# Degrees of a sorted graph from one comparison a group, and the edge loads of the last two groups on another queue

## The chip, the cores and the metric

The kernel runs on one core of one Trainium2 chip. A core has TensorE (PE in the profile, PEld its weight loads), VectorE (DVE), ScalarE (ACT), GpSimd (POOL) and SyncE (SP, which here only starts transfers). SP, ACT and POOL each own a queue on which transfers are issued; all transfers run on the core's 16 DMA engines. The metric is the device time of one execution in microseconds (us), lower is better; several executions are timed and their median counts.

## What is computed

Three graph convolutions with ReLU on 6250 nodes of 256 features and 100000 edges, then a residual sum and a layer norm. `src` and `dst` come sorted by `dst`.

```python
def _gcn_layer(h_in, W, b, src, dst, norm_edge, n_nodes):
    h = h_in @ W
    msg = h[src] * norm_edge[:, None]
    agg = jax.ops.segment_sum(msg, dst, num_segments=n_nodes)
    return agg + b
...
deg = jax.ops.segment_sum(jnp.ones_like(dst, dtype=x.dtype), dst, num_segments=n)   # with self loops
dinv = jnp.where(deg > 0, jax.lax.rsqrt(deg), 0.0)
norm_edge = dinv[src] * dinv[dst]
for W, b in ((W1, b1), (W2, b2), (W3, b3)):
    h = jax.nn.relu(_gcn_layer(h, W, b, src, dst, norm_edge, n))
...
x = _layernorm(x + h, axis=-1)
```

The part that matters here is `deg`: the number of edges that end in each node, plus one, and its use `dinv`, by which every row of x is scaled before the first layer can gather rows.

## The kernel before

**Blocks and groups.** The nodes are cut into NB = 50 blocks of Q = 125, and the blocks into NG = 5 groups of GRP = 10. A first part (up to line 1632) finds for each block where its edges start in the sorted list (`starts`). Then `sorted_path` runs. Its opening, the subject here, fills lines 554 to 717: it loads for each block a run of CAP = 2048 edges, 16 a partition (`ed`), counts the degrees of the nodes, scales x by `dinv` and stores the scaled x to a table in DRAM (`tables[0]`, shown as `tab`). After that come three layers, in which POOL gathers rows of the tables by edge (line 1186), PE sums them with one-hot matrices (1213), and counts of edges between blocks are made (`counts`, lines 785, 814, 852) for a dense product (1273).

**How a degree is counted** (`counted(g)`, lines 627 to 671, a generator with three stages). Partition p of a block holds 16 sorted destinations, made relative to the block in `dlo` (629). For each of 126 thresholds v the number of edges with a destination below v is wanted, and degrees are the differences of neighbours (`step`, 655). DVE makes `near` (values cut off at 125, less 128, line 632), its negative (633), `full` (partitions whose last value is below v, line 636) and `begun` (first value below v, line 638), each of the latter two over 128 x 1260 elements. PE then runs three matmuls a block (642 to 644): begun on near, full on minus near, full on ones. What is left in `part_ps` is, for each threshold, the values of the one partition in which the threshold lies; comparing them (649) and summing (651), plus 16 for each full partition (653), gives the count. Stage two ends with the square root on ACT (659). Stage three takes the reciprocal (661), scales the ten blocks of x (665 on DVE for odd blocks from the third group on, 667 on ACT) and issues the stores of five blocks at a time from SP (669, through `by_rows`, two transfers each, line 74).

**The order.** The whole opening is under a manual schedule: each engine runs its instructions in the order of the Python text. The loop at 704 calls, for k = 0 to 6, stage one of group k, stage three of group k - 2, stage two of group k - 1, and between them single steps of `search()`, which finds the windows of edges that the counts of the first layer need (lines 486 to 549; the matmuls 508 and 509, the sums 511, then an indirect load on POOL, line 521, and further DVE steps from 528). Then `in_parts` (673) splits the scaled x of groups three to five into `parts` (ACT line 675, DVE line 676); the first layer needs it, and the loads of biases and weights (1546, 1547, 756) and the stores of `both` (1439) come behind it on SP.

**The queues in the opening.** `load_edges` (559) reads a start into a register (561) and issues one transfer of 16 KB (564). Of each block group, blocks 0 to 3 are on SP, 4 to 7 on ACT, 8 and 9 on POOL; SP and ACT issue 20 of these each, POOL 10. Behind its 20, SP issues the loads of x of groups three to five (682; those of the first two groups are issued by ACT at the start, line 1568), then four small zero rows (688), then the stores. POOL issues two edge loads, then five indirect loads of edges beyond the 2048 of a block (`beyond`, line 609, used by `rest_counted` 613 in stage two of the first group), then the other eight edge loads.

Of the kernel before, what the change touches and what calls it, by code (L numbers as in the profile page):

```python
# [10 lines left out]
F32 = mybir.dt.float32  # L11
F32R = mybir.dt.float32r
BF16 = mybir.dt.bfloat16
# [9 lines left out]
P = 128  # L23
# [373 lines left out]
def sorted_path(ctx: ExitStack, tc: tile.TileContext, x, edges, starts, found, wts, biases, room, late, out):  # L397
# [156 lines left out]
    with tc.tile_pool(name="sdeg1", bufs=1) as dp1, tc.tile_pool(name="sdeg", bufs=2) as dp, \  # L554
# [17 lines left out]
        base_i = dp1.tile([P, NB], I32, name="base_i")  # L572
        low_i = dp1.tile([P, 2], I32, name="slow_i")
        low = dp1.tile([P, 2], F32, name="slow")
        ones_b = dp1.tile([P, 1], BF16, name="ones_b")
        step = dp1.tile([P, Q], F32, name="step")
        eps = const.tile([P, 1], F32, name="seps")
        zero = dp1.tile([1, HID], F32, name="szero")
# [3 lines left out]
        hot_rest = dp1.tile([P, NG, Q], BF16, name="hot_rest")  # L582

        def numbers():
            nc.gpsimd.iota(low_i, pattern=[[-P, 2]], base=0, channel_multiplier=1)
            nc.gpsimd.iota(base_i, pattern=[[Q, NB]], base=0, channel_multiplier=0)
            nc.gpsimd.iota(keys_i, pattern=[[1, G * NB]], base=0, channel_multiplier=0)
            make_identity(nc, same)
            nc.gpsimd.iota(own_i, pattern=[[0, 1]], base=0, channel_multiplier=G)
            nc.gpsimd.memset(ones_b, 1.0)  # L590
            nc.gpsimd.memset(eps, EPS)
            nc.gpsimd.memset(zero, 0.0)
            nc.vector.tensor_copy(low, low_i)
# [33 lines left out]
        def counted(g):  # L627
            gs = slice(g, g + GRP)
            nc.vector.tensor_tensor(dlo[:, gs, :KF], ed[:, gs, :, 1],
                                    base_i[:, gs].unsqueeze(2).to_broadcast([P, GRP, KF]), op=ALU.subtract)  # L630
            near = dp.tile([P, 2, GRP, KF], BF16, name="near")
            nc.vector.tensor_scalar(near[:, 0], dlo[:, gs, :KF], float(Q), float(P), op0=ALU.min, op1=ALU.subtract)
            nc.vector.tensor_scalar(near[:, 1], near[:, 0], -1.0, None, op0=ALU.mult)
            every = cols[:, :VS].unsqueeze(1).to_broadcast([P, GRP, VS])
            full = dp.tile([P, GRP, VS], BF16, name="sfull")
            nc.vector.tensor_tensor(full, every, dlo[:, gs, KF - 1:KF].to_broadcast([P, GRP, VS]), op=ALU.is_gt)
            begun = dp.tile([P, GRP, VS], BF16, name="begun")
            nc.vector.tensor_tensor(begun, every, dlo[:, gs, 0:1].to_broadcast([P, GRP, VS]), op=ALU.is_gt)
            part_ps = psd.tile([VS, GRP, KF], F32, name="part_ps")
            full_ps = psd.tile([VS, GRP], F32, name="full_ps")  # L640
            for b in range(GRP):
                nc.tensor.matmul(part_ps[:, b, :], lhsT=begun[:, b, :], rhs=near[:, 0, b, :], start=True, stop=False)
                nc.tensor.matmul(part_ps[:, b, :], lhsT=full[:, b, :], rhs=near[:, 1, b, :], start=False, stop=True)
                nc.tensor.matmul(full_ps[:, b:b + 1], lhsT=full[:, b, :], rhs=ones_b, start=True, stop=True)
            yield
            if g == 0:
                rest_counted()
            below = dp.tile([VS, GRP, KF], F32, name="sbelow")
            nc.vector.tensor_scalar(below, part_ps, low[:VS, 1:2], None, op0=ALU.is_lt)
            n_part = dp.tile([VS, GRP], F32, name="n_part")  # L650
            nc.vector.reduce_sum(n_part, below, axis=mybir.AxisListType.X)
            n_below = dp.tile([VS, GRP], F32, name="n_below")
            nc.vector.scalar_tensor_tensor(n_below, full_ps, float(KF), n_part, op0=ALU.mult, op1=ALU.add)
            deg_ps = psd.tile([Q, GRP], F32, name="sdeg_ps")
            nc.tensor.matmul(deg_ps, lhsT=step[:VS, :], rhs=n_below, start=True, stop=False)
            nc.tensor.matmul(deg_ps, lhsT=hot_rest[:, g // GRP, :], rhs=member[:, gs], start=False, stop=True)

            root = dp.tile([Q, GRP], F32, name="sroot")
            nc.scalar.activation(root, deg_ps, AF.Sqrt, bias=1.0)
            yield  # L660
            nc.vector.reciprocal(dinv[:, gs], root)
            v = x_of(g)
            for b in range(GRP):
                if g >= 2 * GRP and b % 2:
                    nc.vector.tensor_scalar(v[:, b, :], v[:, b, :], dinv[:, g + b:g + b + 1], None, op0=ALU.mult)
                else:
                    nc.scalar.activation(v[:, b, :], v[:, b, :], AF.Copy, scale=dinv[:, g + b:g + b + 1])
                if b % 5 == 4:
                    by_rows(nc.sync, v[:, b - 4:b + 1, :],
                            tables[0][(g + b - 4) * Q:(g + b + 1) * Q, :].rearrange("(b p) c -> p b c", p=Q), store=True)  # L670
            yield
# [4 lines left out]
            nc.vector.tensor_sub(parts[:, gs, C:], x_of(g), parts[:, gs, :C].bitcast(F32))  # L676

        with tc.manual_schedule():
            load_edges(SP, nc.sync, [g + b for g in range(0, NB, GRP) for b in range(4)])
            load_edges(ACT, nc.scalar, [g + b for g in range(0, NB, GRP) for b in range(4, 8)])  # L680
            for g in range(2 * GRP, NB, GRP):
                load_x(nc.sync, x_of(g), g)
            numbers()
            load_edges(POOL, nc.gpsimd, range(8, GRP))
            beyond()
            load_edges(POOL, nc.gpsimd, [g + b for g in range(GRP, NB, GRP) for b in range(8, GRP)])
            for table in (*tables, both_halves):
                nc.sync.dma_start(out=table[N:N + 1, :], in_=zero[:, :table.shape[1]])
            nc.vector.tensor_copy(cols, keys_i[:, :P])
            nc.vector.tensor_copy(ident_r, same)  # L690
            nc.vector.tensor_copy(loops, same)
            nc.vector.tensor_sub(step, ident[:, 1:Q + 1], ident[:, 0:Q])
            nc.vector.tensor_copy(own0, own_i)
            idle_slots = 0

            def search():
                nonlocal idle_slots
                if idle_slots > 0:
                    idle_slots -= 1
                else:  # L700
                    idle_slots = next(searches) // 2

            stages = [counted(g) for g in range(0, NB, GRP)]
            for k in range(NG + 2):
                for g in (k, k - 2, k - 1):
                    if 0 <= g < NG:
                        next(stages[g])
                        if k > 0:
                            search()
                if k == NG - 1:  # L710
                    nc.vector.tensor_copy(src, ed[:, :, :, 0])
            while not seen:
                next(searches)
            for g in range(2 * GRP, NB, GRP):
                in_parts(g)
            late_w()
            nc.vector.tensor_copy(keys, keys_i)
# [960 lines left out]
```

## Time and profile before

| | |
|---|---|
| median of 3 runs | 2073.05 us (2067.38 to 2081.36) |
| the profiled execution's own time | 2076.16 us |
| its span, first to last instruction | 2074.4 us |
| busy share: PE, DVE, POOL, ACT | 93%, 72%, 68%, 63% |
| mean granted TensorE clock | 0.961 |
| first gather of the first layer (POOL, line 1186) | starts at 72.95 us |
| first product of a gathered row (PE, line 1213) | starts at 88.14 us |

All sums are made against one profiled execution, whose time is 2076.16 us; that is 3.1 us above the median of the three runs. Times inside the trace are counted from the start of its span. In the rows, the first number is the start and the second the duration in us; what stands in square brackets is how long the engine was idle before, and what ended that.

### The profile page before, as it was taken

What the parts mean: (1) busy time and instruction counts of PE and PEld (TensorE: products, weight loads), DVE (VectorE), ACT (ScalarE), POOL (GpSimd) and SP (SyncE); (2) the same over time, 40 slices, a digit from 0 to 9 for tenths busy, and PEclk for the clock granted to TensorE, in tenths of its full rate; (3) what the DMA queues carried; (4) which work ended last, traced back from release to release, by engine and by line L of the source; (5) the groups of instructions that cost most, each with busy time, mean ns of one, the idle gap of its engine ahead of it and who ended that gap; (6) DMA issues with size and microseconds to landing.
All of it is one profiled execution on the core that took longest, in us unless ns stands there. A gap on an engine that the chain in (4) does not pass through costs nothing. (4 is left out here: it accounts for less than half of the span.)

```text
span 2074.4 us, 30032 instructions
## 1 busy us (share of the span) xinstructions
PE 1923.9 (93%) x8642; PEld 1513.7 (73%) x8642; DVE 1494.1 (72%) x2809; ACT 1302.3 (63%) x2484; POOL 1418.2 (68%) x1442
## 2 busy tenths in 40 slices
PE   4399999999999688999999999999989899999996
PEld 3277777777776467778888878887767777777774
DVE  6877888888882376777766777677675467777776
ACT  2576777787884465766766656667565455556553
POOL 2467777766777377777776776677674577777775
PEclk6699999999999899999999999999999999999998
DMA  7898999999999999999999998978886466666674
GB/s 172 244 308 212 271 260 256 276 260 257 275 274 252 264 268 248 269 260 265 261 262 258 258 260 239 266 230 266 244 239 189 115 180 183 182 178 190 174 191 117
DMA packets 233624, 486.17 MB, mean 234 GB/s; under 512 B 44142, under 2 KB 87358, under 8 KB 233446
## 3 DMA queue, kind: packets, MB, share of 16 engines
q0 software_dynamic: 125184, 315.61, 54.6%
q1 hardware_dynamic: 94980, 159.23, 27.9%
q10 hardware_dynamic: 13282, 9.30, 1.7%
q8 instruction: 70, 1.15, 0.2%
q14 instruction: 108, 0.88, 0.1%
HBM read 416.51 MB, written 67.47 MB: 233 GB/s over the span
## 5 line engine op out<-in xcount | busy, mean ns | idle before, releaser
L1186 POOL DMA_INDIRECT room<-tab,ssrc x1008 | 1025.8, 1018 | 384.6 <-issue 162.6
L1243 DVE TENSOR_TENSOR halves<-room,halves 128x512 fp32r<-128x512 f32 (+1 forms) x806 | 453.4, 579 | 279.0 <-ACT halves L1240 273.0
L1240 ACT CAST halves<-room 128x512 fp32r<-128x512 f32 (+1 forms) x806 | 408.5, 528 | 286.0 <-DMA room<-tab,ssrc 244.7
L1213 PE MATMUL sacc<-halves,shot 128*125 128x512 f32 x1541 | 527.1, 406 | 38.8 <-DVE shot L1136 27.8
L1186 POOL DMA_INDIRECT halves<-both,ssrc x384 | 360.5, 939 | 143.3 <-issue 41.8
L1213 PEld LDWEIGHTS sacc<-halves,shot 128*125 128x125 f32 x1541 | 286.9, 188 | 120.4 <-ACT halves L1240 25.1
L785 DVE TENSOR_TENSOR room<-near_cols,slots 128x625 bf16<-128x625 f32 (+2 forms) x435 | 325.3, 804 | 30.8 <-PE sacc L852 12.7
L1145 ACT CAST piece<-room 125x625 fp32r<-125x625 uint8 x416 | 297.2, 722 | 70.4 <-PE win_ps L1273 19.2
L1136 DVE TENSOR_TENSOR shot<-near_cols,sdlo 128x500 fp32r<-128x500 f32 x371 | 248.0, 670 | 9.3 <-PE sacc L1213 4.8
L1366 PE MATMUL win_ps<-room,w_sb 128*128 128x250 f32 (+1 forms) x832 | 192.5, 375 | 1.6 <-ACT room L1372 1.6
L1273 PE MATMUL win_ps<-parts,piece 125*125 125x512 f32 x650 | 186.2, 405 | 6.2 <-ACT piece L1145 6.2
L1273 PE MATMUL smm<-parts,piece 125*125 125x512 f32 x655 | 188.9, 405 | 1.3 <-ACT piece L1145 0.7
L1366 PEld LDWEIGHTS win_ps<-room,w_sb 128*128 128x128 f32 x832 | 158.0, 195 | 25.3 <-ACT room L1372 2.0
L1273 PE MATMUL mat_ps<-parts,piece 125*125 125x512 f32 x600 | 172.4, 404 | 1.3 <-ACT piece L1145 1.3
L852 PEld LDWEIGHTS <-room 128*125 128x125 bf16 x725 | 95.8, 138 | 74.0 <-issue 23.0
L1273 PE MATMUL sacc<-parts,piece 125*125 125x512 f32 x450 | 147.6, 432 | 0.9 <-ACT piece L1145 0.9
L1273 PEld LDWEIGHTS win_ps<-parts,piece 125*125 125x125 f32 x650 | 119.3, 188 | 37.7 <-ACT piece L1145 8.0
L814 ACT CAST room<-sacc 125x500 uint8<-125x500 f32 (+1 forms) x155 | 107.6, 712 | 56.5 <-PE sacc L852 41.7
L1273 PEld LDWEIGHTS smm<-parts,piece 125*125 125x125 f32 x655 | 116.8, 187 | 29.3 <-issue 2.3
L936 DVE TENSOR_TENSOR parts<-parts 125x512 fp32r<-125x512 f32 x150 | 103.4, 689 | 41.6 <-ACT parts L934 41.6
L1273 PEld LDWEIGHTS mat_ps<-parts,piece 125*125 125x125 f32 x600 | 107.6, 186 | 29.4 <-ACT piece L1145 3.0
L1243 DVE TENSOR_TENSOR parts<-room,parts 128x512 fp32r<-128x512 f32 x138 | 93.4, 692 | 33.3 <-ACT parts L1240 32.9
(310 smaller groups left out, 2938.5 us busy)
## 6 DMA issues: line engine op xcount, KB each, us to landing
parts<-tab SPq DMA_DIRECT2D x81, 448.0 KB
kept<-room SPq DMA_DIRECT2D x29, 683.6 KB
room<-kept SPq DMA_DIRECT2D x29, 683.6 KB
tab<-st SPq DMA_DIRECT2D x74, 224.0 KB
room<-tab,ssrc POOLq DMA_INDIRECT x1008
both<-parts SPq DMA_DIRECT2D x10, 1120.0 KB
own_row<-tab SPq DMA_DIRECT2D x38, 224.0 KB
parts<-kept SPq DMA_DIRECT2D x60, 136.7 KB
```

Source lines behind the costliest of these rows:

```text
L785: nc.vector.tensor_tensor(out, near_cols[:, :shape[2]].unsqueeze(1).to_broadcast(shape), numbers.unsqueeze(2).to_broadcast(shape), op=ALU. ...
L814: nc.scalar.copy(place[:, :, u * G:(u + len(ms)) * G].rearrange("p k (t r) -> p t k r", r=G), counted_in[:Q, :len(ms) * 256].rearrange("p ...
L852: nc.tensor.matmul(bank[:Q, len(pair) * 256:][:, :G * NB], lhsT=hot_lo, rhs=hot_key, start=True, stop=True)
L936: nc.vector.tensor_sub(to[:, HID:], row, to[:, :HID].bitcast(F32))
L1136: nc.vector.tensor_tensor(hot[:, :n], near_cols[:, :Q].unsqueeze(1).to_broadcast([P, n, Q]), dlo.rearrange("p b j -> p (b j)")[:, at:at + ...
L1145: convert(piece, made_or_read[:, c * PIECE:(c + 1) * PIECE, :])
L1186: nc.gpsimd.indirect_dma_start(out=row, out_offset=None, in_=table, in_offset=bass.IndirectOffsetOnAxis(ap=at, axis=0))
L1213: nc.tensor.matmul(acc[:Q, :size], lhsT=hot, rhs=row[:, c0:c0 + size], start=(i == 1 and k == c0 == 0), stop=(k == KF and c0 + size == row ...
L1240: nc.scalar.copy(halves[:, :width], landed[chunk - hi_lag])
L1243: nc.vector.tensor_sub(halves[:, width:], landed.pop(chunk - lo_lag), halves[:, :width].bitcast(F32))
L1273: nc.tensor.matmul(acc_d[:Q], lhsT=got[done // PIECE][:, k % PIECE, :], rhs=parts[:, k], start=(k == 0), stop=(k == NB - 1))
L1366: nc.tensor.matmul(h_ps[:, f, :], lhsT=w2_sb[:, k, (f2 + f) * P:(f2 + f + 1) * P], rhs=zt[:, k, :], start=(k == 0), stop=(k == KH - 1))
```

## The change

It has two parts.

*The count.* `full`, the negative of `near` and the third matmul of each block go. `near` is now the values cut off at 125, plus 1. A new 128 x 128 matrix `shift` (ones on the diagonal, minus ones beside it, first column special) turns, in one matmul for the whole group (`rise_ps`), the values of all partitions into their rises over the partition before. DVE copies these rises from PSUM to a bf16 tile `steps_of[...]`, which has a 17th column of ones for each block. One matmul a block, `begun` on the 17 columns, then sums the rises of all partitions that have begun; the sum is the values of the last of them, and the 17th column counts the partitions. `shift` and the ones are made once.

*The queues.* SP and ACT issue the edge loads of the first three groups only (12 each instead of 20), so that SP's loads of x come behind the third group's edges. POOL issues blocks 8 and 9 of the first two groups (4 loads), then the five indirect loads, then blocks 28 and 29 and all twenty blocks of the last two groups (22 loads).

```diff
@@ constants
-        ones_b = dp1.tile([P, 1], BF16, name="ones_b")
+        shift = dp1.tile([P, P], BF16, name="shift")
+        steps_of = [dp1.tile([P, GRP, KF + 1], BF16, name=f"steps_of{n}") for n in range(2)]
...
-            nc.gpsimd.iota(low_i, pattern=[[-P, 2]], base=0, channel_multiplier=1)
+            nc.gpsimd.iota(low_i, pattern=[[1, 2]], base=0, channel_multiplier=1)
...
-            nc.gpsimd.memset(ones_b, 1.0)
+            for rises in steps_of:
+                nc.gpsimd.memset(rises[:, :, KF:], 1.0)
@@ counted(g)
-            near = dp.tile([P, 2, GRP, KF], BF16, name="near")
-            nc.vector.tensor_scalar(near[:, 0], dlo[:, gs, :KF], float(Q), float(P), op0=ALU.min, op1=ALU.subtract)
-            nc.vector.tensor_scalar(near[:, 1], near[:, 0], -1.0, None, op0=ALU.mult)
+            near = dp.tile([P, GRP, KF], BF16, name="near")
+            nc.vector.tensor_scalar(near, dlo[:, gs, :KF], float(Q), 1.0, op0=ALU.min, op1=ALU.add)
             every = cols[:, :VS].unsqueeze(1).to_broadcast([P, GRP, VS])
-            full = dp.tile([P, GRP, VS], BF16, name="sfull")
-            nc.vector.tensor_tensor(full, every, dlo[:, gs, KF - 1:KF].to_broadcast([P, GRP, VS]), op=ALU.is_gt)
             begun = dp.tile([P, GRP, VS], BF16, name="begun")
             nc.vector.tensor_tensor(begun, every, dlo[:, gs, 0:1].to_broadcast([P, GRP, VS]), op=ALU.is_gt)
-            part_ps = psd.tile([VS, GRP, KF], F32, name="part_ps")
-            full_ps = psd.tile([VS, GRP], F32, name="full_ps")
+            rise_ps = psd.tile([P, GRP, KF], F32, name="rise_ps")
+            nc.tensor.matmul(rise_ps, lhsT=shift, rhs=near, start=True, stop=True)
+            rises = steps_of[g // GRP % 2]
+            nc.vector.tensor_copy(rises[:, :, :KF], rise_ps)
+            part_ps = psd.tile([VS, GRP, KF + 1], F32, name="part_ps")
             for b in range(GRP):
-                nc.tensor.matmul(part_ps[:, b, :], lhsT=begun[:, b, :], rhs=near[:, 0, b, :], start=True, stop=False)
-                nc.tensor.matmul(part_ps[:, b, :], lhsT=full[:, b, :], rhs=near[:, 1, b, :], start=False, stop=True)
-                nc.tensor.matmul(full_ps[:, b:b + 1], lhsT=full[:, b, :], rhs=ones_b, start=True, stop=True)
+                nc.tensor.matmul(part_ps[:, b, :], lhsT=begun[:, b, :], rhs=rises[:, b, :], start=True, stop=True)
...
-            nc.vector.scalar_tensor_tensor(n_below, full_ps, float(KF), n_part, op0=ALU.mult, op1=ALU.add)
+            nc.vector.scalar_tensor_tensor(n_below, part_ps[:, :, KF], float(KF), n_part, op0=ALU.mult, op1=ALU.add)
@@ the loads
-            load_edges(SP, nc.sync, [g + b for g in range(0, NB, GRP) for b in range(4)])
-            load_edges(ACT, nc.scalar, [g + b for g in range(0, NB, GRP) for b in range(4, 8)])
+            first_groups = range(0, 3 * GRP, GRP)
+            load_edges(SP, nc.sync, [g + b for g in first_groups for b in range(4)])
+            load_edges(ACT, nc.scalar, [g + b for g in first_groups for b in range(4, 8)])
             for g in range(2 * GRP, NB, GRP):
                 load_x(nc.sync, x_of(g), g)
             numbers()
-            load_edges(POOL, nc.gpsimd, range(8, GRP))
+            load_edges(POOL, nc.gpsimd, [g + b for g in (0, GRP) for b in range(8, GRP)])
             beyond()
-            load_edges(POOL, nc.gpsimd, [g + b for g in range(GRP, NB, GRP) for b in range(8, GRP)])
+            load_edges(POOL, nc.gpsimd, [*range(2 * GRP + 8, NB)])
...
+            nc.vector.tensor_copy(shift[:, 0:1], same[:, 0:1])
+            nc.vector.tensor_sub(shift[:, 1:], same[:, 1:], same[:, :P - 1])
```

More of the change, by code (lines that the diff above doesn't have):

```diff
@@ L648, in counted @@
             below = dp.tile([VS, GRP, KF], F32, name="sbelow")
-            nc.vector.tensor_scalar(below, part_ps, low[:VS, 1:2], None, op0=ALU.is_lt)
+            nc.vector.tensor_scalar(below, part_ps[:, :, :KF], low[:VS, 1:2], None, op0=ALU.is_lt)
             n_part = dp.tile([VS, GRP], F32, name="n_part")
```

## The prediction

> **What bounds the kernel now.** I read the page first, then the stretches, then the engines in order of time up to 92 us.
>
> ```profile
> span 2074.4 us, 30032 instructions
> PE 1923.9 (93%) x8642; PEld 1513.7 (73%) x8642; DVE 1494.1 (72%) x2809; ACT 1302.3 (63%) x2484; POOL 1418.2 (68%) x1442
> ...
> PE   4399999999999688999999999999989899999996
> ```
>
> Each digit of the last line is a slice of 52 us. From the third slice on PE is nearly full: the layers are bound there and the change does not touch them. Only the first 90 us can move, and what moves there shifts everything behind it once. So the question is what ends the opening last.
>
> ```profile
> 20.00:25.00 5.00, 2.84 (x27) 2.84 (x28) 2.11 (x2) 0.00 (x0) 4.39 (x5) 0.50 0.42 42
> 31.00:50.20 19.20, 15.13 (x109) 13.60 (x110) 16.47 (x38) 9.01 (x24) 0.00 (x0) 0.50 1.04 233
> 50.20:68.30 18.10, 7.20 (x42) 5.76 (x42) 13.09 (x42) 14.52 (x24) 1.30 (x1) 0.50 0.95 289
> 72.00:90.00 18.00, 4.58 (x14) 3.40 (x15) 16.87 (x21) 3.55 (x5) 12.69 (x10) 0.50 0.97 296
> ```
>
> These are stretches: length, busy us of PE, PEld, DVE, ACT, POOL, then granted clock, DMA share, GB/s. Up to 31 us the DMA engines are half empty, behind that they are full, and DVE is busy 86% of 31 to 50. Two chains run side by side. The first is SP's:
>
> ```profile
> 13.71 16.60 SPq L564 DMA_DIRECT2D ed<-in_edges  x20
> 30.36 3.90 SPq L76 DMA_DIRECT2D room<-in_x  x4
> 34.31 6.03 SPq L76 DMA_DIRECT2D last_x<-in_x  x2
> 64.23 4.03 SPq L74 DMA_DIRECT2D tab<-last_x  x4
> 71.92 11.89 SPq L74 DMA_DIRECT2D both<-parts  x6
> ...
> SPq L74 <- DMA last_x<-in_x: 5.4, 1, 5.4
> ...
> L74 SPq DMA_DIRECT2D tab<-room x14: 310/760/1615, 50.2 to 63.6; - x14
> ```
>
> Twenty edge loads take SP 0.83 us each (16.60 / 20); the loads of x start only behind them. One store then waits 5.4 us for the last load of x to land, and from 50.2 us all further stores run with full DMA engines. The last is issued at 68.3. POOL's first gather follows it:
>
> ```profile
> 72.95 2.14 POOL L1186 DMA_INDIRECT room<-tab,rest  x1 [17.75 <-DMA b_sb<-in_L_gnn_b]
> 75.40 0.95 POOL L1186 DMA_INDIRECT room<-tab,ssrc  x1 [0.30 <-issue]
> ...
> 88.14 1.19 PE L1213 MATMUL mat_ps<-room,shot 128*125 128x256 f32 x2 [4.29 <-DMA room<-tab,ssrc]
> ...
> 91.19 2.24 DVE L785 TENSOR_TENSOR room<-near_cols,slots 128x625 bf16<-128x625 f32 x3 [2.09 <-PE str L852]
> ```
>
> PE waits for the gathered row, and DVE then waits 2.09 us for PE: where the chains meet, SP's is the later one by about 2.1 us. The second chain is DVE's:
>
> ```profile
> 27.19 0.33 DVE L629 TENSOR_TENSOR sdlo<-ed,base_i 128x160 f32<-128x160 int32 x1 [5.09 <-DMA ed<-in_edges]
> 46.37 0.33 DVE L629 TENSOR_TENSOR sdlo<-ed,base_i 128x160 f32<-128x160 int32 x1 [0.30 <-issue]
> 60.69 0.23 DVE L528 TENSOR_SCALAR w_sb<-w_sb 125x128 f32<-125x128 int32 x1 [0.66 <-DMA w_sb<-in_edges,w_sb]
> 65.94 5.56 DVE L676 TENSOR_TENSOR parts<-room,parts 125x2560 fp32r<-125x2560 f32 x2 [2.34 <-ACT parts L675]
> ```
>
> At 27.19 it waits for edges of the second group; the fifth group's count starts at 46.37.
>
> **The change part by part.**
>
> ```profile
> L636 DVE TENSOR_TENSOR sfull<-scols,sdlo 128x1260 bf16<-128x1260 f32 x5 | 7.3, 1465 | 0.0
> L633 DVE TENSOR_SCALAR near<-near 128x160 bf16<-128x160 bf16 x5 | 1.0, 202 | 0.2
> L649 DVE TENSOR_SCALAR sbelow<-part_ps,slow 126x160 f32<-126x160 f32 x5 | 1.8, 365 | 0.0
> L692 DVE TENSOR_TENSOR step<-ident_r 128x125 f32<-128x125 f32 x1 | 0.3, 286 | 0.0
> L643 PE MATMUL part_ps<-near,sfull 128*126 128x16 bf16 x50 | 12.7, 254 | 0.0
> L852 PE MATMUL sacc<-room 128*125 128x250 bf16 x34 | 8.2, 308 | 16.8 <-DVE room L785 16.4 <-DVE w_sb L513 0.3
> ```
>
> *DVE.* Each group loses `full` (1.465 us) and the negative of near (0.202), together 1.67. It gains one copy of 128 x 160 out of PSUM; the nearest row is 649, the same size out of PSUM, 0.365. Net 1.3 us a group. The copy needs the rise matmul, which needs only `near`; `begun` (the same shape as `full`) runs meanwhile and covers it. If PE were late, the copy would wait at most for what is queued on PE. The two instructions that build `shift` (row 692 once, and a column) lie before the first edges; so do POOL's two small memsets for one. I cost them at nothing; without that cover they would add some 0.5 us.
>
> *PE.* Per group 30 matmuls become 10 of 17 columns and one of 160. That one is bounded by 0.254 and 0.308; I take 0.3. PE is not the bound there; it shortens the wait for the root by about 0.7 us behind the last groups.
>
> *SP and ACT.* Eight loads of 0.83 us go: x starts 6.65 us earlier, at 23.7. The DMA engines have room there (share 0.42). Against it, 22 loads of 16 KB, 0.36 MB, now run beside x instead of before it: at 233 GB/s 1.5 us. So x has landed, and the stores flow, 5 us earlier (bounds 0 and 6.65; the full gain if the loads fit into gaps). ACT's eight loads hide: its next work comes later.
>
> *POOL.* Here is the price.
>
> ```profile
> 15.50 0.74 POOL L564 DMA_DIRECT2D ed<-in_edges  x1 [0.48 <-issue]
> 16.46 0.56 POOL L564 DMA_DIRECT2D ed<-in_edges  x1 [0.22 <-issue]
> 17.33 1.01 POOL L609 DMA_INDIRECT rest<-in_edges,place_i  x1 [0.31 <-issue]
> 19.98 1.56 POOL L609 DMA_INDIRECT rest<-in_edges,place_i  x1 [0.30 <-issue]
> 24.16 4.35 POOL L564 DMA_DIRECT2D ed<-in_edges  x8
> 53.90 1.30 POOL L521 DMA_INDIRECT w_sb<-in_edges,w_sb  x1 [25.39 <-DVE w_sb L518]
> ...
> L561 POOLq TENSOR_LOAD <-starts x6: 282/288/297, 18.9 to 23.6; - x6
> L564 POOL DMA_DIRECT2D ed<-in_edges x2: 602/610/617, 24.2 to 24.7; - x2
> L564 POOL DMA_DIRECT2D ed<-in_edges x2: 599/600/602, 27.4 to 27.9; - x2
> ```
>
> The eight loads in a row took 0.54 us each, but only since their registers had been read ahead while POOL worked on the indirect loads: those reads stand 0.94 us apart (18.9 to 23.6, five steps), as the first two loads do (15.50, 16.46). So 0.94 is the pace of a long run. Four loads first delay the indirect ones by 2 x 0.96, to 19.25; reads for the 22 begin 1.57 later (18.9 - 17.33), at 20.8, and the last read is at 20.8 + 21 x 0.94 = 40.5; a hold-up of the read-ahead, some 0.5, and 1.0 from read to start, 0.6 for the load: issued by 42.6. The twelfth, the fourth group's last, is out by about 33. How long a load then needs is bounded by 1.9 us (the second of the eight ended at 25.3, DVE went on at 27.19, DMA engines half empty) and 5.5 (the indirect load of line 521, out at 55.2, used at 60.69, DMA engines full). The fifth group's count can start between 44.5 and 48.1. I take the middle, 46.3: the same as the 46.37 of before, since x is still landing but nearly done. All earlier gains of DVE, at the second group's edges (now before the indirect loads on POOL) and 1.3 a group, end in this wait. Behind `beyond`, `rest_counted` gets its rows 1.9 us later, which is covered: the second group's edges are there at 13.71 + 8 x 0.83 + 1.9 = 22.2 instead of 27.19. What is left for DVE is the last group's 1.3 and 0.7 behind it: 2.0 us.
>
> *Sum.* SP's chain gains 5.0, DVE's 2.0; at 91.19 SP's was later by 2.09, so the meeting point gains min(5.0, 2.0 + 2.09) = 4.1, taken as 4. The profiled execution becomes 2076.2 - 4 = 2072; it lay 3.1 above the median of the runs, so the median becomes 2069.
>
> *A rule weighed.* The loads at 27.4 and 27.9 ran beside DVE's instructions of the second group and took 0.600, as long as those at 24.2; the indirect load at 19.98, beside `full`, took 1.56 for 1.01. The Trainium skill, page "SBUF — State Buffer", section "SBUF: two separate sides", speaks against the change: a transfer issued from GpSimd has its descriptors written by GpSimd, which VectorE can lock out, so that 620 ns become about 3100. By its figure each load that meets such an instruction would add some 2.5 us (an estimate); the plain loads here show none of it, the indirect one does.
>
> **The rivals.**
> *All of it (0.15).* The 22 loads go at 0.54 and land in 1.9: then DVE gains over 6 and SP's 6.65 decides: 2073.05 - 6.65 = 2066. Against it stand the 0.94.
> *Nothing (0.2).* VectorE holds up plain loads as it did the indirect one: three `begun` of 1.47 lie in the run, so the last load comes 4.4 us later, the fifth group starts at 50.7, DVE loses 46.37 - 50.7 + 2.0 = -2.3, and its 2.09 of slack is used up: 2073. The same comes out where x gains nothing because full DMA engines only move the wait; for that speaks the share of 1.04, against it the empty stretch at 20 us. That rule of the Trainium skill is what this rival would bear out.
> *Slower (0.15).* The loads land as late as the first gathered rows: out at 76.35, used at 88.14, 11.8 us behind full DMA engines. The fifth group starts at 54.4, DVE loses 8.0 - 2.0 = 6.0, less the slack 2.1: slower by 4, 2077. It decides from a landing 8 us after 42.6, that is a start after 50.5. Against it: the loads of x, which fill the engines, have landed by about 45.
> The forecast, gain of 2 to 5.5, has 0.5.
>
> **How the numbers follow.** The likeliest is 2069, its own range 2067.5 to 2071. The range for 8 in 10 reaches down to 2066 less the 5.7 by which the lowest run lay below the median, 2060.3, taken as 2061, and up to the slow rival, 2077, and 2 for the runs' spread: 2079. A measurement of this kernel tells about 1% (21 us) from no change; no case gives that. Faster by over 1%: 0.03, within 1%: 0.94, slower by over 1%: 0.03, the tails being what I have not seen.
>
> **What would show it.** SP's loads of x starting at 23.7; the next stores flowing from about 45; POOL's edge loads 0.94 apart and out at about 42; the fifth count on DVE at 46; the first gather near 68, the first gathered product near 83 to 84. It is wrong if POOL's run ends before 39 or after 47, if DVE waits for a rise copy, or if the first product moves by 4 and the end does not.

## The result, and the profile after

| | before | after |
|---|---|---|
| median of 22 runs each | 2073.59 us (2065.78 to 2083.13) | 2079.14 us (2071.45 to 2088.18) |
| ratio of the times | 1 | 1.0028, 95% interval 1.0017 to 1.0040 |
| first gather of the first layer (POOL) | 72.95 us | 76.03 us |
| first product of a gathered row (PE) | 88.14 us | 92.12 us |

The changed kernel is slower by 0.28%, 5.8 us (3.5 to 8.3). The forecast was a gain of 4. The profile of the changed kernel begins, by the page:

```profile
span 2073.7 us, 29834 instructions
...
PE   2399999999999789999999999999979899999996
PEclk9999999999999899999999999999999999999998
```

The span is 0.7 us shorter than that of the profile before although the median is 5.5 us longer. Single executions of the changed kernel lie up to 17 us apart (2071.45 to 2088.18), so the ends of these two traces can't be set side by side. The openings can: what bounds them are waits and transfers. By stretch (length, busy us of PE, PEld, DVE, ACT, POOL, then clock, DMA share, GB/s), first one stretch of before that the prediction doesn't show, then after:

```profile
25.00:31.00 6.00, 0.67 (x7) 0.58 (x7) 3.74 (x8) 0.00 (x0) 3.51 (x7) 0.50 0.46 64
```

```profile
25.00:31.00 6.00, 0.94 (x9) 0.84 (x8) 0.63 (x2) 0.00 (x0) 4.86 (x8) 1.00 1.04 234
31.00:50.20 19.20, 6.94 (x34) 5.47 (x35) 9.40 (x28) 6.52 (x18) 8.01 (x15) 1.00 0.96 211
50.20:68.30 18.10, 4.16 (x24) 3.49 (x22) 11.39 (x40) 12.19 (x26) 2.39 (x4) 1.00 0.74 213
72.00:90.00 18.00, 2.72 (x10) 2.01 (x10) 17.68 (x15) 4.51 (x3) 11.83 (x8) 1.00 0.77 224
```

Two numbers say most of it. DVE was busy for 16.47 of the 19.20 us from 31 to 50.2 and is now for 9.40. The DMA engines are full earlier, from 25 us on (0.46 before, 1.04 now), but from 50.2 to 68.3, where they were full with stores, their share falls from 0.95 to 0.74. The opening has new holes. DVE in order of time (start, duration, operation, and in brackets the idle time before it and what ended it), first the use of `rest` in the profile before, which ended no wait, then after:

```profile
31.56 0.24 DVE L616 TENSOR_TENSOR sdlo<-rest,base_i 128x50 f32<-128x50 int32 x1
```

```profile
22.43 0.33 DVE L631 TENSOR_TENSOR sdlo<-ed,base_i 128x160 f32<-128x160 int32 x1 [1.43 <-DMA ed<-in_edges]
...
34.89 0.24 DVE L618 TENSOR_TENSOR sdlo<-rest,base_i 128x50 f32<-128x50 int32 x1 [9.22 <-DMA rest<-in_edges,place_i]
...
45.63 0.33 DVE L631 TENSOR_TENSOR sdlo<-ed,base_i 128x160 f32<-128x160 int32 x1 [4.35 <-DMA ed<-in_edges]
...
54.77 0.33 DVE L631 TENSOR_TENSOR sdlo<-ed,base_i 128x160 f32<-128x160 int32 x1 [5.38 <-DMA ed<-in_edges]
...
72.09 5.56 DVE L676 TENSOR_TENSOR parts<-room,parts 125x2560 fp32r<-125x2560 f32 x2 [2.34 <-ACT parts L675]
```

The second group's count starts 4.8 us earlier (27.19 before), as wanted. Then DVE stands still three times: 9.2 us for the rows beyond a block's 2048 (`rest`), 4.35 us for the fourth group's edges, 5.4 us for the fifth's. The fifth count starts at 54.77 instead of 46.37, `parts` at 72.09 instead of 65.94. All three waits are for transfers that POOL issues:

```profile
19.38 2.27 POOL L611 DMA_INDIRECT rest<-in_edges,place_i  x1 [0.30 <-DVE near L634]
...
23.23 2.00 POOL L611 DMA_INDIRECT rest<-in_edges,place_i  x1 [0.30 <-issue]
...
26.78 0.94 POOL L611 DMA_INDIRECT rest<-in_edges,place_i  x1 [0.30 <-issue]
27.73 2.75 POOL L564 DMA_DIRECT2D ed<-in_edges  x5
32.60 0.54 POOL L564 DMA_DIRECT2D ed<-in_edges  x1 [2.12 <-DMA rest<-in_edges,place_i]
34.12 0.53 POOL L564 DMA_DIRECT2D ed<-in_edges  x1 [0.98 <-DMA rest<-in_edges,place_i]
...
51.57 0.53 POOL L564 DMA_DIRECT2D ed<-in_edges  x1 [0.40 <-issue]
```

The last indirect load is out at 27.72 (26.78 + 0.94), but its rows are used at 34.89: 7.2 us. From the sixth of the 22 edge loads on POOL itself waits: that load is released by the landing of an indirect load, the third of the five, eight transfers before it. The run ends at 52.10, not at 42.6. SP's rows:

```profile
13.90 9.55 SPq L564 DMA_DIRECT2D ed<-in_edges  x12
23.50 4.64 SPq L76 DMA_DIRECT2D room<-in_x  x4
28.18 6.30 SPq L76 DMA_DIRECT2D last_x<-in_x  x2
...
42.70 23.16 SPq L74 DMA_DIRECT2D tab<-room  x16
66.23 3.99 SPq L74 DMA_DIRECT2D tab<-last_x  x4
...
78.07 10.98 SPq L74 DMA_DIRECT2D both<-parts  x6
```

The loads of x start at 23.50 instead of 30.36. Yet the stores end later (66.23 + 3.99 = 70.2; 68.3 before), and the next view of the same queue, its waits (total, times, longest), says why:

```profile
SPq L74 <- ACT room L667: 10.1, 4, 4.5
SPq L74 <- DVE room L665: 5.2, 2, 4.8
...
SPq L74 <- DMA last_x<-in_x: 0.7, 1, 0.7
```

Before, a store waited 5.4 us for x to land; now the stores wait 0.7 us for x, and their longest waits (4.5 and 4.8 us) are for rows of x that ACT and DVE have not scaled yet, since the degrees come late.

### The profile page after: what moved, and what is told of

Read it like the earlier page. It is cut to its first block, busy times and chain, and to the rows that moved or that the text cites. A ratio compares the mean times of both kernels' runs of the same rounds, so it can differ in the third digit from the quotient of the medians.

```text
span 2073.7 us, 29834 instructions
## 1 busy us (share of the span) xinstructions
PE 1913.9 (92%) x8547; PEld 1503.1 (72%) x8547; DVE 1487.4 (72%) x2806; ACT 1303.2 (63%) x2484; POOL 1430.1 (69%) x1459
## 4 chain that ended last, share of the span: by engine, by line
PE 34%; DMA 12%; issue 8%; DVE 5%; POOL 4%; ACT 2%; ACTq 1%; DVEq 0%; POOLq 0%; SPq 0%
DMA room<-tab,ssrc 12%; PE sacc L1216 9%; PE win_ps L1369 5%; POOL room L1189 4%; PE win_ps L1276 4%; PE smm L1276 3%; PE mat_ps L1276 3%; PE win_ps L1382 3%; DVE halves L1246 2%; PE sacc L982 2%; PE smm L982 2%; PE mat_ps L982 2%; PE str L982 2%; ACT halves L1243 1%; DVE shot L1139 1%
## 5 line engine op out<-in xcount | busy, mean ns | idle before, releaser
L1369 PEld LDWEIGHTS win_ps<-room,w_sb 128*128 128x128 f32 x832 | 156.1, 193 | 26.5 <-ACT room L1375 3.1
L1276 PEld LDWEIGHTS smm<-parts,piece 125*125 125x125 f32 x655 | 117.4, 188 | 30.6 <-issue 2.3
```

Source lines behind the costliest of these rows:

```text
L1276: nc.tensor.matmul(acc_d[:Q], lhsT=got[done // PIECE][:, k % PIECE, :], rhs=parts[:, k], start=(k == 0), stop=(k == NB - 1))
L1369: nc.tensor.matmul(h_ps[:, f, :], lhsT=w2_sb[:, k, (f2 + f) * P:(f2 + f + 1) * P], rhs=zt[:, k, :], start=(k == 0), stop=(k == KH - 1))
```

## The experiments

Two theories were set against each other. Theory 1: what POOL issues while x is on its way lands late, so DVE's waits come from the neighbourhood of x. Theory 2: POOL's pace is the cause (a register read of 0.94 us a load, in one long run), whatever is beside it. In the table, "fifth count" is the start of the last group's subtraction on DVE, "product" the first product of a gathered row; all in us but the ratio, which is to before on the same chip.

| | `rest` used | POOL's run out | fifth count | product | ratio, 95% interval |
|---|---|---|---|---|---|
| before | 31.6 | 28.5 | 46.4 | 88.14 | 1 |
| after | 34.9 | 52.1 | 54.8 | 92.12 | 1.0028 (1.0017 to 1.0040) |
| e1_count | 30.6 | 28.7 | 42.4 | 86.48 | 0.9984 (0.9963 to 1.0005) |
| e2_queues | 34.0 | 51.0 | 52.6 | 91.92 | 1.0037 (1.0015 to 1.0059) |
| e3_x_held | 28.2 | 44.4 | 51.4 | 89.84 | 1.0012 (0.9988 to 1.0036) |
| e4_rest_first | 26.4 | 45.5 | 48.7 | 87.71 | 1.0011 (0.9986 to 1.0036) |
| e5_shared | 26.3 | 34.5 | 45.7 | 84.25 | 0.9981 (0.9963 to 0.9998) |
| e6_between | 26.3 | 27.4 | 42.0 | 90.92 | 1.0004 (0.9989 to 1.0019) |
| e7_fixed | 33.3 | 46.3 | 48.6 | 85.60 | 0.9990 (0.9973 to 1.0007) |
| e8_spread | 27.3 | 33.5 | 41.6 | 83.31 | 0.9988 (0.9971 to 1.0005) |
| e9_both | 31.2 | 46.9 | 50.0 | 87.20 | 0.9995 (0.9975 to 1.0015) |
| e10_x_far | 29.2 | 43.8 | 45.5 | 99.69 | one run, not compared |
| e11_spread_again | 26.2 | 31.4 | 41.1 | 85.60 | 0.9985 (0.9968 to 1.0002) |

The runs of before beside e8_spread and e9_both took 2345 us, so their ratios go by that. All columns but the ratio come from one profiled execution each: e8 and e11 are the same kernel, and their products lie 2.3 us apart. e7 and e9 leave out the starts of 22 blocks and so work on other edges there; their openings can be read, their ratios only with that in mind.

### The two halves: e1_count and e2_queues

e1 is the new count with the queues of before, e2 the new queues with the count of before.

```diff
 e1, against after
-            first_groups = range(0, 3 * GRP, GRP)
-            load_edges(SP, nc.sync, [g + b for g in first_groups for b in range(4)])
+            load_edges(SP, nc.sync, [g + b for g in range(0, NB, GRP) for b in range(4)])
...
 e2, against before: only the five lines of the loads
```

> The new count with the queues of before. If the loss is all in the queues: the fifth group's count on DVE starts at 41 to 43 us instead of 46.4, x still lands at 50, so SP's chain stays the later one and the first gathered product only moves from 88.1 to 87 to 88; time between 3 us faster and equal. If the new count itself costs (the copy of the rises waits for PE, or PE's extra step is late): DVE idles ahead of that copy and the time is 3 us or more slower.

> The new queues with the count of before. If the loss is all in the queues: the fifth count starts at 54 to 56 us and the time is 5 to 8 us slower than before, since the saved instructions of DVE lie in front of its waits. If part of the loss came from the new count: slower by 1 to 4 only.

The count alone is 0.16% faster (3.3 us; the interval just holds 1), the queues alone 0.37% slower (7.7 us, 3.1 to 12.2), both about as expected; e2's fifth count, at 52.6, came earlier than the 54 to 56 expected. First e1's row of the fifth count, then, from e2's timeline, the same waits as after:

```profile
42.37 0.33 DVE L631 TENSOR_TENSOR sdlo<-ed,base_i 128x160 f32<-128x160 int32 x1 [0.30 <-DMA room<-in_x]
```

```profile
34.04 0.24 DVE L616 TENSOR_TENSOR sdlo<-rest,base_i 128x50 f32<-128x50 int32 x1 [7.46 <-DMA rest<-in_edges,place_i]
...
52.59 0.33 DVE L629 TENSOR_TENSOR sdlo<-ed,base_i 128x160 f32<-128x160 int32 x1 [1.56 <-DMA ed<-in_edges]
```

With the old queues the fifth count starts 4.0 us earlier, and the product moves only by 1.7: SP's last store came 0.6 us earlier (66.9 for 67.5) and its chain holds the product, as the prediction read at the meeting point; DVE's `parts` came some 5.5 us earlier (60.39 for 65.94) and did not bring the product with it. With the new queues the product is at 91.92 with the slow count and at 92.12 with the fast one. What the new count saves, DVE then spends in waiting. So the loss belongs to the queues.

### Is it x? e3_x_held and e10_x_far

Both are the changed kernel with more loads of block 0's edges on SP ahead of x: 8 (x starts at 30.7), and 24 (x starts at 43.7, behind nearly all of POOL's run).

```diff
+            load_edges(SP, nc.sync, [0] * 8, again)      # e3; [0] * 24 in e10
             for g in range(2 * GRP, NB, GRP):
                 load_x(nc.sync, x_of(g), g)
```

> The changed kernel, but SP loads block 0 eight times more into a spare tile between its edges and x, so that x starts at about 30.4 us as before; POOL's loads are those of the changed kernel. Theory 1 (small transfers of POOL land late when they run beside x): DVE's wait of 9.2 us for the rows of the indirect loads falls under 3, the third count starts at 31 to 33 instead of 38.2, the fifth at 48 to 51, and the time is near before, 0 to 4 slower. Theory 2 (POOL's own pace, with x innocent): the fifth count stays at 53 to 55 and, as x is later by 6.7 as well, the time is 5 to 8 slower than before. Work is added: eight loads of 16 KB that nothing reads.

> The changed kernel with 24 loads more on SP ahead of x (of block 0's edges, into a tile that nothing reads; this work is added, and so x is late), so that x starts near 43.7 us instead of 23.5 and nothing large is in flight while POOL loads. Theory 1 (the wait is for landings beside x): rest's rows are used at 27 to 28 instead of 34.9, POOL's 22 loads follow one another at the pace of their register reads, 22 x 0.66 to 0.94 from 27, so the run ends between 42 and 47 instead of 52.1, no load of it waits over 1 us for an earlier one's landing, and the fifth group's edges are counted at 44 to 49 instead of 54.8. Theory 2 (POOL's own pace of issue is the whole cause): the run ends at 52 and the fifth count is at 54 to 55 all the same. By either the kernel is slower than the changed one, 8 us or more, since x's last stores come some 10 to 20 us later; the time isn't what this run is for.

e10's POOL and DVE rows:

```profile
26.70 0.95 POOL L613 DMA_INDIRECT rest<-in_edges,place_i  x1 [0.30 <-issue]
27.64 7.12 POOL L566 DMA_DIRECT2D ed<-in_edges  x13
...
43.27 0.54 POOL L566 DMA_DIRECT2D ed<-in_edges  x1 [0.40 <-issue]
```

```profile
29.16 0.25 DVE L620 TENSOR_TENSOR sdlo<-rest,base_i 128x50 f32<-128x50 int32 x1 [3.59 <-DMA rest<-in_edges,place_i]
...
45.45 0.33 DVE L633 TENSOR_TENSOR sdlo<-ed,base_i 128x160 f32<-128x160 int32 x1 [4.70 <-DMA ed<-in_edges]
```

The same instructions of POOL in the same order: the rows of the last indirect load are used 1.5 us after it is out (27.65 to 29.16) instead of 7.2, thirteen edge loads follow one another without a wait, the run ends at 43.8 instead of 52.1, the last load is used 1.6 us behind that, the fifth count starts at 45.45 instead of 54.77. Theory 2 gave 52 and 54 to 55 here and falls as the whole cause; `rest` came 1 us later than theory 1 had it. The pace is real, and with it alone the run ends at 43.8; the 8.3 us behind that come only with x beside the run.

e3 shows both in one trace, first POOL's last load, then DVE:

```profile
43.83 0.53 POOL L566 DMA_DIRECT2D ed<-in_edges  x1 [0.40 <-issue]
```

```profile
28.16 0.25 DVE L620 TENSOR_TENSOR sdlo<-rest,base_i 128x50 f32<-128x50 int32 x1 [2.28 <-DMA rest<-in_edges,place_i]
...
51.39 0.33 DVE L633 TENSOR_TENSOR sdlo<-ed,base_i 128x160 f32<-128x160 int32 x1 [6.90 <-DMA ed<-in_edges]
```

`rest`, issued ahead of x, is used 1.5 us after the last of its loads is out (25.75 + 0.95); the last edge load, beside x and the first stores, 7.0 us after. Its fifth count missed theory 1's 48 to 51 by 0.4 us. The product comes 2.3 us ahead of after's.

Where the time of a late transfer goes can be seen in the transfers by queue. From 26 to 30 us, in after and then in e10 (packets and rate; queue, packets, MB, share; q1 is SP's, q0 POOL's):

```profile
DMA packets 1112, 1.13 MB, mean 283 GB/s; under 512 B 22, under 2 KB 1110, under 8 KB 1110
...
q1 hardware_dynamic: 1108, 1.11, 107.0%
...
q0 software_dynamic: 2, 0.00, 0.3%
```

```profile
DMA packets 735, 0.11 MB, mean 28 GB/s; under 512 B 702, under 2 KB 734, under 8 KB 734
...
q0 software_dynamic: 158, 0.04, 13.5%
```

In these 4 us the last two indirect loads of POOL came out and five edge loads were started in both kernels. In e10 its queue moved 158 packets, in after 2 of 1112. The transfers don't finish late, they start late, while nearly all packets are x's. Whether the DMA engines keep to SP's queue or POOL's requests reach them late, this view doesn't tell. DVE isn't what holds them: in after it is idle from 25.66 to 34.89.

### Taking the loads out of x's way: e4_rest_first, e7_fixed, e9_both

e4 puts the indirect loads back behind two edge loads. e7 loads POOL's 22 blocks from fixed places, without a register read. e9 does both.

```diff
 e4: blocks 18 and 19 to SP and ACT
-            load_edges(POOL, nc.gpsimd, [g + b for g in (0, GRP) for b in range(8, GRP)])
+            load_edges(POOL, nc.gpsimd, range(8, GRP))
 e7
-            load_edges(POOL, nc.gpsimd, [*range(2 * GRP + 8, NB)])
+                for b in range(2 * GRP + 8, NB):
+                    nc.gpsimd.dma_start(out=ed[:, b], in_=edges[b * 2000:b * 2000 + CAP, :].rearrange("(p j) t -> p j t", p=P))
```

> The changed kernel, but the five indirect loads stand in POOL's queue where they were before, behind two edge loads; blocks 18 and 19 go to SP and ACT, one each, which puts x 0.8 us later. Theory 1: their rows are out before x starts, DVE's wait of 9.2 us falls under 4, the third count starts at 30 to 33; POOL's 22 loads start 3 us earlier but still run beside x, the fifth count starts at 50 to 52, and the time is 0 to 3 slower than before. Theory 2 (POOL's pace of 0.94 a load alone decides): the same start of the fifth count, 50 to 52, for another reason, and the waits between POOL's loads stay under 0.5 us throughout. If VectorE's comparisons hold POOL up: the indirect loads beside a comparison again take 2.0 to 2.3 us.

> The changed kernel, but POOL's 22 loads take their edges from fixed places (2000 times the block) instead of the blocks' starts, so that POOL reads no register between them: the edges of 22 blocks and what follows from them are not the reference's. Theory 1 (late landing beside x): POOL's loads are issued faster, but the rows of the indirect loads stay as late as in the changed kernel (DVE's wait of 9 us), and the fifth count starts at 50 to 53; time 2 to 6 slower than before. Theory 2 (the pace of 0.94): without it the 22 loads take 12 to 13 us, the fifth count starts at 43 to 46, and the time is equal to before or faster.

> The changed kernel with both of the edits that each took about 6 us off the fifth count: the indirect loads in their old place (18 and 19 on SP and ACT), and POOL's 22 loads from fixed places without register reads; the edges of 22 blocks and what follows are not the reference's. If late rows (through POOL's later loads, which wait for them) and the reads are separate costs, they add up: the fifth count starts at 42 to 44, and DVE waits under 4 us for edges in all; first gathered product at 82 to 84. If both edits only relieved the same wait (the loads' landing beside x), the fifth count stays at 47 to 49.

e4 takes the wait for `rest` away (used at 26.4), and the fifth count comes 6 us earlier than after's, also earlier than the 50 to 52 of both theories; a new wait of 8.7 us stands ahead of the fourth group's edges, which now run beside x. POOL waits for landings up to 2.5 us between loads, where theory 2 had under 0.5. The product ends level with before's. e7 keeps the wait for `rest`, and its run, with no register to read, still isn't paced by POOL:

```profile
32.73 0.54 POOL L689 DMA_DIRECT2D ed<-in_edges  x1 [2.91 <-DMA rest<-in_edges,place_i]
...
40.44 0.54 POOL L689 DMA_DIRECT2D ed<-in_edges  x1 [2.59 <-DMA ed<-in_edges]
```

22 loads of 0.54 would take 12 us; they take 20 (26.5 to 46.3), held by landings. Its fifth count, 48.6, lies between the two theories, and the ratio of 0.9990 is not the 2 to 6 us slower of theory 1: the register reads cost something as well.

e9 can't tell whether the two edits add. Its fifth count is 50.0, outside both expectations, but e4's edit was undone in it: two of the indirect loads ran into DVE's comparison and took 2.20 and 1.95 us, the last was out at 25.74, behind the start of x at 25.01 (24.14 and 24.56 in e4), and `rest` was used at 31.2 instead of 26.4.

Part of the 8.3 us remains unexplained. After's load that starts at 43.34 is 6.3 us behind the same load of e10 (37.03), the last one 8.3. From 43 to 51 us the starts of after's loads lie up to 2.0 us apart, one register read there takes 1.32 us where 0.29 is the median, and no landing is named as the releaser. Without the reads (e7) this part is shorter; what slows a read beside x is open.

### Other shares: e5_shared, e6_between, e8_spread and e11_spread_again

All have the new count and `rest` in its old place. e5 leaves POOL 11 of the late loads and gives ACT 11, with x from 24.4; e8, and e11 which is the same, spread them over SP (16 in all), ACT (20) and POOL (14), with x at 27; e6 leaves POOL six and puts SP's late edge loads between two loads of x.

```diff
 e5
+            load_edges(SP, nc.sync, [*range(4), *range(10, 14), 18, *range(20, 24)])
+            load_edges(ACT, nc.scalar, [*range(4, 8), *range(14, 18), 19, *range(24, 28), *range(30, 35), *range(40, 46)])
...
+            load_edges(POOL, nc.gpsimd, [28, 29, *range(35, 40), *range(46, NB)])
 e6
+            load_x(nc.sync, x_of(2 * GRP), 2 * GRP)
+            load_edges(SP, nc.sync, [*range(30, 34), *range(40, 44)])
```

> The new count; the indirect loads in their old place; x from SP at 24.6 us; the 22 edge loads behind them shared out, 11 on POOL and 11 on ACT (half of the fourth group, six of the fifth). Theory 1a (small loads beside x land late on any queue): ACT's last load is out at 34, POOL's at about 36, and DVE still waits for edges, the fifth count starting at 43 to 47. Theory 1b (late on POOL's queue above all): the same, since POOL's half is late. Theory 2 (POOL's pace): half the run, so the fifth count starts as soon as DVE gets there, at 39 to 42, with no wait over 1 us. Time: 1 to 3 faster than before under theory 1, 4 to 6 faster under theory 2.

> The new count; the indirect loads in their old place; SP loads the third group's x between its edges of the third and of the fourth group, the other two groups' x behind all edges; POOL loads six blocks behind the indirect loads. Theory 1: only 1.25 MB of x run beside the small loads, so DVE waits less than 3 us for edges or rows in all after the second group; the fifth count starts at 41 to 44; x has landed by 46 to 47 instead of 50, and the time is 3 to 5 faster than before. Theory 2 gives the same fifth count; if x beside the edges cost nothing, more of x could be put there and this kernel would not beat e5_shared.

> The new count; the indirect loads in their old place; edges spread so that each queue has few loads behind x's start: SP 16 (blocks 28, 30 and 31 too), ACT 20 (29, 32 to 35, 40, 41 too), POOL 14 (36 to 39 and 42 to 49); x starts at 27.2 us. If late landing beside x and POOL's long run are both what cost, the fifth count starts at 41 to 44, ACT's first root is not held up by loads, x has landed by 47 to 48, and the first gathered product comes at 83 to 85: 3 to 6 us faster than before, at least as fast as the new count alone. If only POOL's run mattered, the fifth count would start no later than 41.

> The kernel e8_spread once more, unchanged, beside the others' kernel before on another chip: new count, POOL's share of the late edges cut to 12 behind rest's rows in their old place, SP 16 and ACT 20 loads, x at 27.2. In e8_spread its first product came 4.8 us earlier than before's and the ratio was 0.9988 with an interval that holds 1. Theory 1 (what the opening gains at the first product is kept to the end): 3 to 6 us faster than before, ratio 0.997 to 0.9985. Rival (the 4.8 us is given back later, as the page of the whole run can't tell): within 1 us of before, ratio 0.9995 to 1.0005.

e5 is the one version whose interval lies below 1, if barely (3.9 us faster than before, 0.4 to 7.7); its fifth count, 45.7, is theory 1's. Its price shows on ACT, which works only when its 24 loads are issued. But e5 also moved x, as SP's row shows:

```profile
13.84 23.99 ACTq L564 DMA_DIRECT2D ed<-in_edges  x24
37.94 0.18 ACT L659 ACTIVATE sroot<-sdeg_ps 125x10 f32<-125x10 f32 x1 [29.68 <-issue]
```

```profile
24.39 12.15 SPq L76 DMA_DIRECT2D room<-in_x  x4
```

These four transfers took 4.64 us in after. Here SP waits 9.1 us between the second and the third, by its waits for the landing of an edge load, so two thirds of x go out from 34.8 on, behind nearly all edges. So e5 doesn't show that the shares alone bring the gain. In e8 and e11 the last third of x is issued late too, at 35.3 and 35.6.

e8 and e11 have the earliest fifth counts of the versions that bring x forward, 41.6 and 41.1, and ratios of 0.9988 and 0.9985. Each interval just holds 1, but two separate comparisons agree on some 3 us, the lower end of the 3 to 6 expected. The product came 4.8 us earlier in e8 and 2.5 in e11. e6 missed its 3 to 5 us. Its fifth count is as early as e8's, but its SP rows say:

```profile
24.35 1.64 SPq L76 DMA_DIRECT2D room<-in_x  x2
33.63 6.71 SPq L564 DMA_DIRECT2D ed<-in_edges  x8
40.39 1.07 SPq L76 DMA_DIRECT2D room<-in_x  x2
```

Between the first load of x (issued by 26.0) and SP's next edge load lie 7.6 us in which SP starts nothing, and the rest of x is held with it, to 40.4. The waits of SP name the landing of an edge load as the end of 6.9 us of this, and the semaphore (the counter by which a landing is told) is that of an edge load of ACT, issued at 26.14 beside x and landed at 33.61; SP goes on at 33.63. In the traces SP's and ACT's transfers take turns at eight semaphores, POOL's at eight others, and a transfer starts only when the last one with its semaphore has landed. So a small load of ACT lands late beside x too, 7.1 us behind its issue, and it can hold up SP. From 31 to 50 the DMA engines are busy for 0.61 only.

Over all compared runs the first product and the whole time go together: where the product moved by -4.8 to -1.7 us the measured ratio is below 1, where it moved by +1.7 to +4.0 it is above, and e4 and e9 lie between (-0.4 and -0.9 us, 1.0011 and 0.9995). Only for after, e2 and e5 does the interval leave out 1. As far as these runs can tell, what the opening gains or loses at its end is kept.

## Why the prediction was wrong, point by point

*What bounds the kernel, and the meeting point: right.* The layers are full, the opening shifts them once, and of two chains the later counts. e1 bears out that SP's chain was the later: 4.0 us at the fifth count became 1.7 at the product.

*The count: right.* By the groups of the profile after (busy us and mean ns):

```profile
L637 DVE TENSOR_TENSOR begun<-scols,sdlo 128x1260 bf16<-128x1260 f32 x5 | 7.3, 1465 | 0.0
L641 DVE CAST steps_of<-rise_ps 128x160 bf16<-128x160 f32 x5 | 1.6, 323 | 0.0
...
L639 PE MATMUL rise_ps<-near,shift 128*128 128x160 bf16 x5 | 1.5, 298 | 15.6 <-DVE near L634 15.6
```

The copy took 0.32 (0.365 taken), the rise matmul 0.30 (0.3 taken), and DVE never waits for it behind `begun`, the zero in the copy's last column. From the fifth count to the last reciprocal of a root DVE takes 9.9 us instead of 12.0 (54.77 to 64.64; 46.37 to 58.37), 2.1 less where 2.0 was taken, though the wait for the last root, 1.11 us, is as long as before (1.12).

*SP's start: right; SP's gain: wrong.* x started at 23.5 (23.7 taken), and the next stores began at 44.7 ("about 45"). But the step "so x has landed, and the stores flow, 5 us earlier" took SP's chain for independent of DVE's. A store needs x and its degree. With DVE late, the stores stood still for 4.6 us up to 50.1 and for 5.5 us up to 58.5, and the chain lost 2 us at its end instead of gaining 5.

*"Behind beyond, rest_counted gets its rows 1.9 us later, which is covered": the first step that failed.* The indirect loads did come out later as worked out, but the rows were used at 34.89 and not near 30, since x was issued at 23.5, ahead of the last of them. The price of landing was taken from the time before, when x started behind them. That moved neighbour, which the same change brought, was priced at 1.5 us of bandwidth for 22 loads. What went wrong is not the count of bytes but the order: 0.36 MB don't add 1.5 us to x, they land late behind x.

*"Issued by 42.6": wrong by 9.5 us, by the same neglect.* The pace of 0.94 was right, and e10, with x out of the way, shows the forecast's run of POOL nearly to the number, 43.8 for its end and 45.5 for the fifth count (42.6 and 46.3 taken). But the landing, bounded by 1.9 and 5.5 us, was charged to the last load alone. It belongs to each, and POOL starts no load until the eighth before it has landed, so late landings of the first stretch the run of all. Of the 8.3 us that after's run ends behind e10's, some 6 are seen to come this way; the other 2, from 43 us on, are open.

*The rivals.* "Slower" had the fifth group at 54.4, 4 us lost and 2077; measured were 54.77, 4.0 us at the product, and 2079.14, just above the range's 2079. Its point of decision (a start after 50.5) held. Its mechanism was half right: small loads do land late behind x, but the first ones did, by 7 us; the last took 2.7 (52.10 to 54.77). The argument against it, that x has landed by about 45, is true only for that last one, and it gave the rival its low chance. "Nothing" had VectorE hold up plain loads. After's 22 took 0.53 to 0.60 us each, those beside `begun` too (two of the three lay in the run, the fifth group's behind it); no plain load was held. The two indirect loads that started at 19.38 and 23.23, within the `begun` of the first and second group, took 2.27 and 2.00, the three others 0.94 to 0.98. So the rule of the Trainium skill, page "SBUF — State Buffer", section "SBUF: two separate sides", is borne out by the indirect loads, with 1.1 to 1.3 us each, and by none of the plain ones; for a VectorE instruction with two inputs in SBUF, as `begun` is, the section itself names only GpSimd operations that read SBUF. The indirect loads are such: the places that they fetch stand in a tile in SBUF.

*A rule on queues that bears on what failed.* The Trainium skill, page "DMA: Bandwidth & Descriptors", section "Queues, rings and completion order", says that a DMA engine takes turns between the queues that have work for it, a whole packet at a time, typically 9 to 17 descriptors and at most 64. By turns of 17 a small load would lose about 1 us beside x (an estimate: 16 engines moved 1108 packets on SP's queue in 4 us, 69 each, if a packet of the trace is a descriptor). The trace doesn't agree: POOL's queue, with seven transfers issued, got two packets in these 4 us, and 7 us are some 120 packets an engine, more than one turn at the page's ceiling. So turns alone don't account for the delay, and no run here shows the length of a turn. Nor is it the same in each run: in e5, in the same 4 us, POOL's queue moved 52 packets and ACT's 162 beside 996 of SP's. The same page's section "Issuing engines are not separate DMA queues" says that all queues end on the same 16 engines, and the trace agrees: to move loads to POOL's queue doesn't move them out of x's way.

## What to carry to other kernels

When a change brings a bulk transfer forward, list every small transfer on any queue that is issued after its new start, and price each one's landing beside it, not the bytes; here that was 7 us instead of 1.5. Where transfers share a few semaphores, late landings turn into late issues, so a long run of small loads beside bulk traffic takes longer than its own pace, and one queue can hold up another (e6). Issue what an in-order engine waits for first ahead of the bulk, spread the rest over the queues (e5, e8; some 3 us here, and only e5's interval leaves out 1), and look in the view by queue whether a late transfer finished late or started late.

## What the runs showed of the hardware

- Small transfers of POOL are used 1.5 to 1.6 us after their issue with nothing large beside them (e10) and 7.0 to 7.2 us after beside x (after, e3). An edge load of ACT beside x landed 7.1 us after its issue (e6).
- In these kernels a transfer is held back until the last one with its semaphore has landed; POOL's take turns at eight, SP's and ACT's together at eight others. In before no wait of POOL for a landing is seen, in e7 it is up to 2.9 us for a load; in e6 a landing of ACT's held up SP for 6.9 us.
- The indirect loads of `rest` take 0.94 to 1.1 us to issue. One that starts while DVE runs the comparison for `begun` ends 0.8 to 0.9 us after that comparison has ended (after: 21.65 for 20.76 and 25.23 for 24.42; e4: 21.64 for 20.82), and so takes up to 2.3 us; one that started together with it, in e7, took 1.01. In after, plain edge loads take 0.53 to 0.60 us beside it or not, the first of all 0.74.
- In the profile before the clock granted to PE was 0.50 from 11 to 93 us, in that of after 1.00 through the opening; from 150 us on both have 0.98. e1 at 0.50 and e5 at 1.00 both have earlier products than before, and e8 at 0.50 has an earlier one than the same kernel e11 at 1.00, so that is not what moved them.
